# A graph-network kernel's carry pass: 86 weight columns in three groups of 32, with a fourth row tile in the fourth column group

## The chip, the cores and the metric

The kernel runs on one core of a Trainium2 chip. The metric is the device time of one execution in microseconds. The kernel before took 1119.12 us (median of 3 runs, 1116.25 to 1122.83).

## What is computed

Four graph layers run one after another on x (2708 nodes, 128 features) and a sparse-valued but densely stored matrix adj (2708 x 2708); each ends with a residual sum and a layer norm. Layer 0 is a Laplacian product with a nearest-neighbour step, layers 2 and 3 are products of adj with the features. The change lies in layer 1, an attention:

```python
XW = jnp.matmul(X, W)
s_col = jnp.matmul(XW, a[0, :f])
s_row = jnp.matmul(XW, a[0, f:])
Z1 = jax.nn.leaky_relu(s_row[:, None] + s_col[None, :], negative_slope=0.01)
den = jnp.exp(Z1)
num = jnp.matmul(A, den)
att = jnp.where(num != 0, den / jnp.where(num != 0, num, 1.0), 0.0)
H = jnp.matmul(A, jnp.matmul(att, XW))
```

Because den is the exponential of a leaky rectifier of r_i + c_j, it is the larger of two products, exp(r_i) exp(c_j) and exp(0.01 r_i) exp(0.01 c_j). Once the columns j are sorted by c_j, each row i has one place at which it changes from one form to the other. The kernel uses this to get num = A @ den without an N x N x N product.

## The kernel before

**Tiling.** The transposed adjacency is read in panels. The 2708 rows are 21 full tiles of 128 and a last one of 20 (FULL = 21, LAST = 20). The columns are six chunks (C = 6): four of 512, one of 384 and one of 276. The last six row tiles stay in SBUF (`res`, RES = 6); the first sixteen (S = 16) are streamed in groups of four by `load_panel` (L157, one DMA of 4 x 128 rows by the chunk's width) into the pool `stream`, which has three buffers with the tag strip. The 20 rows of the last tile are kept at partitions 0, 32 or 64 (`few`, L92), so that three chunks' products with them can use three different row groups of TensorE.

**The order of the work.** A scheduler orders the instructions of each engine by the dependences; the source's order is a hint, and only stretches under `manual_schedule` are kept as written. Each engine then takes its own queue in order. SyncE issues the panel loads; GpSimd issues the scatters, broadcasts and gathers.

**The third pass (L785 to L960), which the change rewrites.** The sorted columns are cut into NB = 43 blocks of 64. For a row that lies wholly on one side of a block, its contribution to that block needs only one of two weights. So lc (L786) holds for each row tile 2 x 43 = 86 weight columns, and the pass multiplies all of adj by them: `by_panels` (L171) goes over the chunks c and the row tiles i, and `product` (L180, the matmul is L186) adds lc of tile i, 128 x 86, times the panel of tile i, 128 x up to 512, into one PSUM bank for the chunk. The outputs use 86 of the 128 columns of the array. When a chunk is done, `end_carry` (L952) copies the bank to `carry`, on VectorE for even chunks and on ScalarE for odd ones (`evacuate`, L151).

**What runs beside it.** GpSimd's queue holds, in this sequence: 22 indirect scatters by_rank (L815), the load of the sorted features xws (L916), 22 scatters by_slot, the product xws * g_col (L936), the load of slots (L930), and two broadcasts of a row to all partitions by `on_all` (L806): g_row and gb. Both take the one buffer with the tag hT, so gb is written only when the last reader of g_row is done. That reader is `listed` (L938): it makes the gather's indices slot_i (L940) and 43 weight tiles lw (L947, one per block, on VectorE) from g_row. `ranked` (L928) is called after chunk 2 and `listed` after chunk 3.

**The own stage (from L989).** After a branch on a flag, for each half h of the columns and each pair of blocks q, GpSimd gathers the rows that change form within a block (L1035, indices slot_i) into a strip buffer; two rows of carry are added by SyncE (L1040); TensorE forms num from rows and lw in two groups of 64 columns (L1048); ScalarE and VectorE turn num into err (L966 to L972, the last with gb); and TensorE adds err times xws into hacc (L977). The gathers stand in GpSimd's queue behind gb, and their strip buffers are those of the panels.

Of the kernel before, what the change touches and what calls it, by code (L numbers as in the profile page):

```python
# [13 lines left out]
ALU = mybir.AluOpType  # L14
# [7 lines left out]
KC = 126  # L22
OOB = 4095
# [5 lines left out]
class Due:  # L29
# [21 lines left out]
def kernel(  # L51
# [16 lines left out]
    nc = tc.nc  # L68
    N, D = x.shape
    assert D == P  # L70
    T = (N + P - 1) // P
# [18 lines left out]
    GROUPS = 3  # L90

    def few(c):  # L92
        g = c % GROUPS * 32
        return slice(g, g + LAST)
# [37 lines left out]
    ident = const.tile([P, P], F32, tag="ident", name="ident")  # L132
# [18 lines left out]
    def evacuate(n, dst, src):  # L151
        if n % 2:
            nc.scalar.copy(dst, src)
        else:
            nc.vector.tensor_copy(dst, src)

    def load_panel(g, c, pool=stream):  # L157

        s = pool.tile([P, 4, CW], F32, tag="strip", name="part")
        nc.sync.dma_start(  # L160
            s[:, :, : cw[c]],
            adjT[g * 4 * P : (g + 1) * 4 * P, cols[c]].rearrange("(t p) k -> p t k", p=P),
        )
        return s
# [6 lines left out]
    def by_panels(weights, done, tick=None, ready=(), first=None, behind=None):  # L171

        ready = list(ready)
        accs = {}

        def product(c, i, src, w):  # L180
            lhsT = weights(i)[few(c) if i == FULL else slice(None)]
            start = c not in accs
            if start:
                accs[c] = acc_tile()
            stop = tick is None and i == (FULL if c % GROUPS == 0 else FULL - 1)
            nc.tensor.matmul(accs[c][: lhsT.shape[-1], :w], lhsT=lhsT, rhs=src, start=start, stop=stop)  # L186

        for c in range(C):
            w = cw[c]
            for i in [*(first if first and c == 0 else range(FULL)), *([FULL] if c % GROUPS == 0 else [])]:  # L190
                if i == FULL:
                    for n in range(c, c + GROUPS):
                        product(n, i, res[few(n), i - S, cols[n]], cw[n])
                    done(c, accs[c])
                    for _ in range(GROUPS if tick is not None else 0):
                        tick()
                    continue
                if i < S:
# [130 lines left out]
    with tc.tile_pool(name="knn", bufs=1) as knn:  # L329
# [96 lines left out]
        with (  # L426
# [5 lines left out]
            for c in range(C):  # L432
# [24 lines left out]
                ts = chunk_tiles[c]  # L457
# [51 lines left out]
        for n, half in enumerate((1, 0)):  # L509
# [3 lines left out]
                op0=ALU.mult, op1=ALU.mult, accum_out=wae[:, D + n : D + n + 1],  # L513
# [272 lines left out]
    lc = lc_pool.tile([P, T, NB, 2], F32, tag="lc", name="lc")  # L786

    with tc.tile_pool(name="rank", bufs=1) as rank:
        def rtile(shape, name, dt=F32):
            return rank.tile([P] + shape, dt, tag=name, name=name)  # L790
# [5 lines left out]
        def as_row(col, name):  # L796

            ps = mis_tile()
            nc.tensor.transpose(ps[:T, :P], col, ident)
            lines = rank.tile([T, P], F32, tag=name, name=name)  # L800
            nc.scalar.activation(lines, ps[:T, :P], AF.Exp, scale=0.99)
            flat = dram.tile([T, P], F32, tag=name + "_d", name=name + "_d")
            nc.gpsimd.dma_start(flat[:, :], lines)
            return flat

        def on_all(name, flat):  # L806
            row = big.tile([P, N], F32, tag="hT", name=name)
            nc.gpsimd.dma_start(row, bass.AP(tensor=flat.tensor, offset=flat.offset, ap=[[0, P], [1, N]]))
            return row
# [51 lines left out]
        with tc.manual_schedule(engines={nc.vector.engine}):  # L861
            for t0, t1 in ((0, 4), (4, half_t), (half_t, T)):
                n = t1 - t0
# [15 lines left out]
        for t0, t1 in halves:  # L879
            n = t1 - t0  # L880
# [11 lines left out]
        for t0, t1 in halves:  # L892
            rhs = in_b[:, t0:t1, :].rearrange("p t b -> p (t b)")
# [10 lines left out]
        pos = rtile([T], "pos")  # L904
# [6 lines left out]
            nc.vector.tensor_copy(val[:, :, n], v)  # L911
        nc.vector.scalar_tensor_tensor(pos, pos, float(NB), blk, op0=ALU.mult, op1=ALU.add)
        pos_u = rtile([T], "pos_u", U32)
        placed = nc.vector.tensor_copy(pos_u, pos).ins
        r_row = as_row(rr, "g_r")
        nc.gpsimd.dma_start(  # L916
            xws[:, : N // P, :], by_rank[: FULL * P, :].rearrange("(q p) d -> p q d", p=P)
# [5 lines left out]
        carry = big.tile([P, N], F32, tag="y", name="carry")  # L923
        slots = rtile([NB, 3], "slots")
        g_row = None


        def ranked():  # L928
            nonlocal g_row
            nc.gpsimd.dma_start(slots.rearrange("p b v -> p (b v)"), by_slot.rearrange("(p b) v -> p (b v)", p=P))  # L930
            with tc.issue_after(placed):
                nc.vector.tensor_copy(csort, xws[:, :, D + 1])
            nc.scalar.activation(g_col, csort, AF.Exp, scale=0.99)
            nc.scalar.activation(g_inv, csort, AF.Exp, scale=-0.99)
            g_row = on_all("g_row", as_row(csort, "g_c"))
            nc.gpsimd.tensor_mul(xws[:, :, :D], xws[:, :, :D], g_col[:, :, None].to_broadcast([P, NQ, D]))  # L936

        def listed():  # L938
            for h in range(2):
                nc.vector.tensor_scalar(  # L940
                    slot_i[h], slots[:, :, 0], 2.0, 2.0 * OOB + h, op0=ALU.mult, op1=ALU.add
                )

            nc.vector.tensor_scalar_add(slot_e, slots[:, :, 1], ident[:, KC : KC + 1])
            nc.vector.tensor_scalar_add(slot_f, slots[:, :, 2], ident[:, KC + 1 : KC + 2])
            for b in range(NB):
                nc.vector.tensor_scalar(  # L947
                    lw[:, b, : bw[b]], g_row[:, b * BJ : b * BJ + bw[b]], slot_e[:, b : b + 1], slot_f[:, b : b + 1],
                    op0=ALU.mult, op1=ALU.max,
                )  # L950

        def end_carry(c, acc):  # L952
            evacuate(c, carry[: 2 * NB, cols[c]], acc[: 2 * NB, : cw[c]])
            if c == 2:
                ranked()
            if c == 3:
                listed()

        by_panels(lambda i: lc[:, i, :, :].rearrange("p b s -> p (b s)"), end_carry)
        gb = on_all("gb", r_row)  # L960

    def mix(w, q, num, col, haccs, pool):
# [27 lines left out]
    with tc.If(over > KC) as full:  # L990

        with (
# [10 lines left out]
            for h in range(2):  # L1003
                hacc = dps.tile([P, 3 * CW], F32, tag="hacc", name="hacc")
                for q in range(NQ):
                    num = dps.tile([P, 3 * CW], F32, tag="num", name="num")
                    for i in range(T):
# [5 lines left out]
                        s = stream.tile([P, HALF], F32, tag="strip", name="part")  # L1013
                        nc.sync.dma_start(s[: pw[i]], adjT[i * P : i * P + pw[i], h * HALF : (h + 1) * HALF])
                        for c0 in range(0, HALF, CW):
# [3 lines left out]
                                start=(i == 0), stop=(i == T - 1),  # L1019
# [3 lines left out]
    with full.Else():  # L1023
        with (
# [4 lines left out]
            for h in range(2):  # L1029
                hacc = ops.tile([P, 3 * CW], F32, tag="hacc", name="hacc")  # L1030
                for q in range(NQ):
                    pair = [b for b in (2 * q, 2 * q + 1) if b < NB]
                    rows = stream.tile([P, 2, HALF], F32, tag="strip", name="rows")
# [9 lines left out]
                    for c0, w, bufs in ((0, WIDE, 2), (WIDE, NARROW, 1)):  # L1043
                        num = ops.tile([P, w], F32, tag=f"num{w}", name="num", bufs=bufs)
                        for o in range(0, w, CW):
                            e = min(w, o + CW)
                            for n, b in enumerate(pair):
                                nc.tensor.matmul(  # L1048
                                    num[n * BJ : n * BJ + bw[b], o:e], lhsT=lw[:, b, : bw[b]],
                                    rhs=rows[:, n, c0 + o : c0 + e], start=True, stop=True,  # L1050
# [9 lines left out]
    for t in range(T):  # L1060
        p = pw[t]
# [41 lines left out]
    for t in range(T):  # L1103
        p = pw[t]
# [59 lines left out]
```

## Time and profile before

| | |
|---|---|
| time, median of 3 | 1119.12 us |
| profiled span | 1119.4 us |
| mean granted TensorE clock | 0.971 |
| PE busy | 1044.2 us (93%) |
| VectorE, ScalarE, GpSimd busy | 642.7, 306.1, 299.4 us |
| first product of the third pass | 445.52 us from the start |
| last product of the third pass ends | 547.65 us |
| first gather of the own stage issued | 541.91 us |
| first hacc product of the own stage | 562.99 us |
| own stage's mT copied | 781.22 us |

A line of the profile names the source line, the engine, the operation and the tiles (out<-in), then partitions x elements and a count. PE is the matmul, PEld the loading of weights beside it, DVE is VectorE, ACT ScalarE, POOL GpSimd and SP SyncE. A float32 product is recorded as two matmul instructions and two weight loads. In a timeline the first number is the start in us from the start of the span and the second the length of the merged piece; the square bracket gives how long the engine had been idle and what ended it.

### The profile page before, as it was taken

How to read it: one execution, taken by the hardware profiler on the slowest of the kernel's cores; microseconds unless marked ns; L12 is line 12 of the kernel's file. 1: busy time of each engine (PE TensorE's matmuls, PEld its weight loads, DVE VectorE, ACT ScalarE, POOL GpSimd, SP SyncE). 2: the span in 40 equal slices, each digit the busy share in tenths (PEclk: the TensorE clock that was granted, in tenths of full speed). 3: DMA queues.
4: the chain of work that ended last, by engine and by line, in shares of the span. 5: the costliest groups of instructions: out<-in, count | busy, mean ns of one | idle time of the engine just before them, and what ended most of it. 6: DMA issues, size and time to landing. Idle time of an engine off the chain costs nothing.

```text
span 1119.4 us, 10743 instructions
## 1 busy us (share of the span) xinstructions
PE 1044.2 (93%) x3495; PEld 494.5 (44%) x3495; DVE 642.7 (57%) x1381; ACT 306.1 (27%) x569; POOL 299.4 (27%) x296
## 2 busy tenths in 40 slices
PE   0899999999999975999799999998999999999997
PEld 0346544444345654333333333333444644465445
DVE  6885549999636679403099999997311212122132
ACT  0000145555202434000165656664110100011000
POOL 4000000000477772772355655660010100000000
PEclk9999999999999995999999999998999999998999
DMA  9996320000576660797545534454475766563754
GB/s 349 354 316 222 125 101 1 1 0 1 178 274 201 184 207 13 230 304 236 164 121 148 176 96 129 164 171 142 150 236 186 227 227 219 173 227 117 263 166 129
DMA packets 110245, 193.89 MB, mean 173 GB/s; under 512 B 14156, under 2 KB 47106, under 8 KB 109926
## 3 DMA queue, kind: packets, MB, share of 16 engines
q1 hardware_dynamic: 91046, 151.12, 40.7%
q0 software_dynamic: 19136, 42.01, 12.0%
q8 instruction: 29, 0.48, 0.2%
q14 instruction: 34, 0.28, 0.1%
HBM read 217.20 MB, written 4.30 MB: 198 GB/s over the span
## 4 chain that ended last, share of the span: by engine, by line
PE 51%; issue 4%; DMA 4%; DVE 2%; POOL 1%; ACT 1%; POOLq 0%; DVEq 0%; ACTq 0%
PE acc L186 32%; PE hacc L977 8%; PE num L1048 8%; DMA rows<-in_adjT,slot_i 2%; DMA part<-in_adjT 1%; PE mis L259 1%; POOL rows L1035 1%; DVE mask L692 1%; PE mis L1110 0%; PE mis L1063 0%; DMA got<-y_rows,where 0%; ACT junk L710 0%; ACT hT L220 0%; PE mis L1076 0%; DVE mask L697 0%
## 5 line engine op out<-in xcount | busy, mean ns | idle before, releaser
L186 PE MATMUL acc<-part,y 128*128 128x512 f32 (+2 forms) x384 | 156.0, 550 | 2.1 <-DMA part<-in_adjT 1.6
L1035 POOL DMA_INDIRECT rows<-in_adjT,slot_i x86 | 120.7, 1404 | 107.9 <-PE num L1048 79.9
L1048 PE MATMUL num<-rows,lw 128*64 128x512 f32 (+2 forms) x516 | 117.0, 558 | 6.7 <-DMA rows<-carry 3.7
L977 PE MATMUL hacc<-err,xws 128*128 128x512 f32 (+3 forms) x264 | 113.6, 567 | 2.2 <-DVE err L972 1.8
L574 PE MATMUL acc<-zT,z 128*128 128x512 f32 (+4 forms) x264 | 106.9, 552 | 0.0
L602 POOL DMA_INDIRECT got<-y_rows,where x88 | 93.0, 1057 | 29.6 <-issue 11.9
L186 PEld LDWEIGHTS acc<-part,y 128*128 128x128 f32 x384 | 70.4, 191 | 64.5 <-issue 53.9
L970 DVE TENSOR_TENSOR err<-inv,num 128x1024 f32<-128x1024 f32 (+1 forms) x88 | 74.5, 856 | 27.1 <-DMA rows<-in_adjT,slot_i 21.0
L966 ACT ACTIVATE inv<-num 128x1024 f32<-128x1024 f32 (+1 forms) x88 | 64.3, 734 | 88.4 <-PE num L1048 86.6
L575 ACT COPY key<-acc 128x512 f32<-128x512 f32 (+3 forms) x132 | 70.2, 534 | 58.1 <-issue 29.8
L392 PE MATMUL acc<-part,y 128*128 128x512 f32 (+2 forms) x192 | 82.4, 582 | 2.2 <-DVE y L233 2.2
L977 PEld LDWEIGHTS hacc<-err,xws 128*128 128x128 f32 (+1 forms) x264 | 47.1, 192 | 80.4 <-issue 41.8
L186 PE MATMUL acc<-part,lc 128*86 128x512 f32 (+2 forms) x192 | 76.2, 553 | 3.3 <-DVE lc L876 2.5
L186 PE MATMUL acc<-part,xs 128*128 128x512 f32 (+2 forms) x192 | 78.6, 552 | 0.1
L972 DVE SCALAR_TENSOR_TENSOR err<-gb,g_inv,err 128x1024 f32<-128x1024 f32 (+1 forms) x88 | 77.1, 918 | 0.0
L536 POOL TENSOR_TENSOR y<-xs,d2inv 128x2176 f32<-128x2176 f32 (+1 forms) x2 | 4.6, 2322 | 264.3 <-ACT d2inv L534 264.3
L186 PE MATMUL acc<-part,mixed 128*128 128x512 f32 (+2 forms) x192 | 75.0, 545 | 0.2 <-DMA part<-in_adjT 0.2
L971 DVE SCALAR_TENSOR_TENSOR err<-err,inv 128x1024 f32<-128x1024 f32 (+1 forms) x88 | 71.8, 857 | 0.0
L574 PEld LDWEIGHTS acc<-zT,z 128*128 128x128 f32 (+1 forms) x264 | 47.0, 186 | 53.8 <-issue 48.4
L220 ACT COPY hT<-acc 128x512 f32<-128x512 f32 (+2 forms) x18 | 9.6, 534 | 220.1 <-PE acc L186 203.2
L967 ACT ACTIVATE inv<-inv 128x1024 f32<-128x1024 f32 (+1 forms) x88 | 67.3, 768 | 2.6
L576 DVE MAX8 near<-key 128x8 f32<-128x2708 f32 (+1 forms) x22 | 65.3, 2970 | 3.4 <-ACT key L575 3.4
(239 smaller groups left out, 1215.5 us busy)
## 6 DMA issues: line engine op xcount, KB each, us to landing
part<-in_adjT SPq DMA_DIRECT2D x102, 1024.0 KB
part<-in_adjT SPq DMA_DIRECT2D x24, 768.0 KB
part<-in_adjT SPq DMA_DIRECT2D x24, 552.0 KB
res<-in_adjT SPq DMA_DIRECT2D x4, 1280.0 KB
got<-y_rows,where POOLq DMA_INDIRECT x88, 3.9
rows<-in_adjT,slot_i POOLq DMA_INDIRECT x86, 5.8
rows<-carry SPq DMA_DIRECT2D x86, 10.6 KB
xws<-by_rank POOLq DMA_DIRECT2D x1, 1365.0 KB, 10.1
```

Source lines behind the costliest of these rows:

```text
L186: nc.tensor.matmul(accs[c][: lhsT.shape[-1], :w], lhsT=lhsT, rhs=src, start=start, stop=stop)
L392: nc.tensor.matmul(accs[c][:, : cw[c]], lhsT=y[:, i, :], rhs=src[:, : cw[c]], start=first, stop=last)
L574: nc.tensor.matmul(pks[c][:p, : cw[c]], lhsT=z2[:, :p], rhs=zT[:, cs], start=False, stop=True)
L575: nc.scalar.copy(key[:p, cs], pks[c][:p, : cw[c]])
L602: nc.gpsimd.indirect_dma_start(out=got[:p, :], out_offset=None, in_=y2_rows[:, :], in_offset=bass.IndirectOffsetOnAxis(ap=where[:p, t, k : ...
L967: nc.scalar.activation(inv[:p], inv[:p], AF.Exp, scale=-1.0)
L970: nc.vector.tensor_mul(err[:p], inv[:p], num[:p, :w])
L971: nc.vector.scalar_tensor_tensor(err[:p], err[:p], 2.0, inv[:p], op0=ALU.subtract, op1=ALU.mult)
L972: nc.vector.scalar_tensor_tensor(err[:p], gb[:p, col : col + w], g_inv[:p, q : q + 1], err[:p], op0=ALU.max, op1=ALU.mult)
L977: nc.tensor.matmul(haccs[:, o:e], lhsT=xws[:p, q, :D], rhs=err[:p, o:e], start=(q == 0), stop=(q == NQ - 1))
L1035: nc.gpsimd.indirect_dma_start(out=rows[:KC, n, :], out_offset=None, in_=adj_half[:, :], in_offset=bass.IndirectOffsetOnAxis(ap=slot_i[h][ ...
L1048: nc.tensor.matmul(num[n * BJ : n * BJ + bw[b], o:e], lhsT=lw[:, b, : bw[b]], rhs=rows[:, n, c0 + o : c0 + e], start=True, stop=True,)
```

## The change

The 86 weight columns are cut into three groups, 32, 32 and 22 wide, each of which goes to its own column group of the array: output partitions 0 to 31, 32 to 63 and 64 to 85. The fourth column group, partitions 96 to 127, is then free, and takes a fourth row tile: while row tiles 1, 2 and 3 of a panel are each multiplied in three groups, one third of the fourth tile goes through the fourth group each time. So four row tiles are meant to take the time of three products. Since the three thirds of the fourth tile all come out at partitions 96 to 127, they need three PSUM banks: the chunk's own and two more, taken from the pool mis.

At the end of a chunk the bank is copied to carry on ScalarE, and VectorE adds the three parts from partitions 96 up. `listed` moves from chunk 3 to chunk 4 and makes only the first 10 of the 43 lw tiles; the other 33 come after the adds of the last chunk. `issue_after` keeps csort, slot_i and lw behind the adds on VectorE.

```diff
-        def listed():
-            for h in range(2):
...
-            for b in range(NB):
+        def listed(added):
+            with tc.issue_after(added):
+                for h in range(2):
...
+            weigh_own(range(NB // 4))
+
+        def weigh_own(blocks):
+            for b in blocks:
                 nc.vector.tensor_scalar(
                     lw[:, b, : bw[b]], g_row[:, b * BJ : b * BJ + bw[b]], slot_e[:, b : b + 1], slot_f[:, b : b + 1],
                     op0=ALU.mult, op1=ALU.max,
                 )
 
-        def end_carry(c, acc):
-            evacuate(c, carry[: 2 * NB, cols[c]], acc[: 2 * NB, : cw[c]])
+        lcs = lc.rearrange("p t b s -> p t (b s)")
+        Q = 32
+        quads = [slice(o, min(o + Q, 2 * NB)) for o in range(0, 2 * NB, Q)]
+        assert len(quads) == 3
+        left = [slice(3 * Q, 3 * Q + q.stop - q.start) for q in quads]
+        banks, begun = {}, set()
+
+        def part_sum(c, i, src, bank, rows, k):
+
+            if (c, bank) not in banks:
+                banks[c, bank] = mis_tile() if bank else acc_tile()
+            nc.tensor.matmul(
+                banks[c, bank][rows, : cw[c]], lhsT=lcs[:, i, quads[k]], rhs=src,
+                start=(c, bank, rows.start) not in begun, stop=False, skip_group_check=True,
+            )
+            begun.add((c, bank, rows.start))
+
+        for c in range(C):
+            for g in range(T // 4 + 1):
+                ts = range(4 * g, min(4 * g + 4, FULL))
+                part = load_panel(g, c) if g < S // 4 else None
+                srcs = [
+                    part[:, i % 4, : cw[c]] if part is not None else res[:, i - S, cols[c]] for i in ts
+                ]
+                for n, i in enumerate(ts[:3]):
+                    for k in range(3):
+                        part_sum(c, i, srcs[n], 0, quads[k], k)
+                    if len(ts) == 4:
+                        part_sum(c, ts[3], srcs[3], n, left[n], n)
+            if c % GROUPS == 0:
+                for n in range(c, c + GROUPS):
...
+            nc.scalar.copy(carry[: 2 * NB, cols[c]], banks[c, 0][: 2 * NB, : cw[c]])
+            for bank, (q, r) in enumerate(zip(quads, left)):
+                added = nc.vector.tensor_add(carry[q, cols[c]], banks[c, bank][r, : cw[c]], carry[q, cols[c]])
             if c == 2:
-                ranked()
-            if c == 3:
-                listed()
-
-        by_panels(lambda i: lc[:, i, :, :].rearrange("p b s -> p (b s)"), end_carry)
+                ranked(added.ins)
+            if c == 4:
+                listed(added.ins)
+            if c == C - 1:
+                with tc.issue_after(added.ins):
+                    weigh_own(range(NB // 4, NB))
         gb = on_all("gb", r_row)
```

More of the change, by code (lines that the diff above doesn't have):

```diff
@@ L913 @@
         pos_u = rtile([T], "pos_u", U32)
-        placed = nc.vector.tensor_copy(pos_u, pos).ins
+        nc.vector.tensor_copy(pos_u, pos)
         r_row = as_row(rr, "g_r")
@@ L925, with ranked @@
         g_row = None
-        def ranked():
+        def ranked(added):
             nonlocal g_row
             nc.gpsimd.dma_start(slots.rearrange("p b v -> p (b v)"), by_slot.rearrange("(p b) v -> p (b v)", p=P))
-            with tc.issue_after(placed):
+            with tc.issue_after(added):
                 nc.vector.tensor_copy(csort, xws[:, :, D + 1])
@@ L936, in ranked @@
             nc.gpsimd.tensor_mul(xws[:, :, :D], xws[:, :, :D], g_col[:, :, None].to_broadcast([P, NQ, D]))
-        def listed():
-            for h in range(2):
[L940 to L945, printed above, removed]
-            for b in range(NB):
+        def listed(added):
+            with tc.issue_after(added):
+                for h in range(2):
+                    nc.vector.tensor_scalar(
+                        slot_i[h], slots[:, :, 0], 2.0, 2.0 * OOB + h, op0=ALU.mult, op1=ALU.add
+                    )
+                nc.vector.tensor_scalar_add(slot_e, slots[:, :, 1], ident[:, KC : KC + 1])
+                nc.vector.tensor_scalar_add(slot_f, slots[:, :, 2], ident[:, KC + 1 : KC + 2])
+            weigh_own(range(NB // 4))
+        def weigh_own(blocks):
+            for b in blocks:
                 nc.vector.tensor_scalar(
@@ new lines @@
+        banks, begun = {}, set()
[5 more added lines that the diff above has]
+                start=(c, bank, rows.start) not in begun, stop=False, skip_group_check=True,
+            )
+            begun.add((c, bank, rows.start))
[13 more added lines that the diff above has]
+                for n in range(c, c + GROUPS):
+                    if n != c:
+                        banks[n, 0] = acc_tile()
+                    nc.tensor.matmul(
+                        banks[n, 0][: 2 * NB, : cw[n]], lhsT=lcs[few(n), FULL, :], rhs=res[few(n), FULL - S, cols[n]],
+                        start=n != c, stop=False, skip_group_check=True,
+                    )
+                    begun.update((n, 0, q.start) for q in quads)
+            nc.scalar.copy(carry[: 2 * NB, cols[c]], banks[c, 0][: 2 * NB, : cw[c]])
+            for bank, (q, r) in enumerate(zip(quads, left)):
+                added = nc.vector.tensor_add(carry[q, cols[c]], banks[c, bank][r, : cw[c]], carry[q, cols[c]])
+            if c == 2:
+                ranked(added.ins)
[4 more added lines that the diff above has]
+                    weigh_own(range(NB // 4, NB))
```

## The prediction

> **What bounds the kernel now.** The page first: PE is busy 93% of the span and the chain that ended last gives PE 51%, so what counts in a stage is whether TensorE works back to back there. Then its list of costly groups, for the group the change rewrites:
>
> ```profile
> L186 PE MATMUL acc<-part,lc 128*86 128x512 f32 (+2 forms) x192 | 76.2, 553 | 3.3 <-DVE lc L876 2.5
> ```
>
> That is the third pass, panel tiles only (the resident tiles are another group). Each product is two instructions. The timeline gives its pace, the windows what TensorE and the DMA engines do meanwhile (columns: stretch, length, busy us of PE, PEld, DVE, ACT, POOL, granted clock, DMA share, GB/s):
>
> ```profile
> 503.93 13.90 PE L186 MATMUL acc<-part,lc 128*86 128x512 f32 x32
> ```
>
> ```profile
> 452.00:468.00 16.00, 16.00 (x44) 5.58 (x43) 9.46 (x29) 1.68 (x5) 12.56 (x12) 1.00 0.91 292
> 468.00:486.00 18.00, 18.00 (x43) 6.53 (x42) 0.82 (x2) 0.33 (x2) 12.38 (x13) 1.00 0.84 278
> 486.00:504.00 18.00, 18.00 (x44) 6.49 (x43) 0.00 (x0) 0.58 (x1) 13.81 (x15) 1.00 0.90 284
> 504.00:523.00 19.00, 19.00 (x49) 6.54 (x47) 4.20 (x19) 0.27 (x1) 6.32 (x4) 1.00 0.78 261
> 548.00:563.00 15.00, 9.46 (x31) 3.04 (x31) 4.60 (x6) 6.91 (x10) 5.24 (x6) 0.89 0.37 107
> ```
>
> TensorE never rests from 452 to 537, but DMA is at 78 to 91% behind it: there is little more speed in this pass before the panels are late. After the pass (its last matmul ends at 547.65) PE does 9.5 us of work in 15 us. So next I read who starts the own stage, in the queue of GpSimd and in the chain:
>
> ```profile
> 513.12 0.55 POOL L808 DMA_DIRECT2D g_row<-g_c_d  x1 [3.34 <-DMA g_c_d<-g_c]
> 529.95 0.54 POOL L808 DMA_DIRECT2D gb<-g_r_d  x1 [16.28 <-DVE lw L947]
> 541.91 1.11 POOL L1035 DMA_INDIRECT rows<-in_adjT,slot_i  x1 [11.42 <-DMA part<-in_adjT]
> ```
>
> ```profile
> 538.73 3.01 DMA part<-in_adjT
> ...
> 541.91 0.38 POOL rows L1035
> ...
> 546.09 11.52 DMA rows<-in_adjT,slot_i
> ```
>
> The first gather waits for the last panel (landed 541.74), and the gathers, not the matmuls of the pass, lead to the first hacc product at 562.99 (timeline of PE), 21.1 us after the gather was issued. One line of the queue matters most: gb stands ahead of the gathers and waits 16.28 us for lw, because gb takes the buffer (tag hT) of g_row, which lw reads. Today lw is over in time:
>
> ```profile
> 520.00 9.65 DVE L947 TENSOR_SCALAR lw<-g_row,slot_e,slot_f 128x64 f32<-128x64 f32 x43 [6.13 <-DMA g_row<-g_c_d]
> ```
>
> **What the Trainium skill says.** "TensorEngine Tiling (Array Packing)", Tiling Modes: four tiles of 128 rows by 32 columns run independently, and a change of mode drains the array. The trace has two and three tiles at once: of the 20-row products of three column chunks, the first passes all start at 466.67 and the second at 467.17; 64-column pairs of num start two by two at 604.47 and 604.90.
>
> ```profile
> 466.67 0.67 PE L186 MATMUL acc<-res,lc 20*86 20x512 f32 x3
> ```
>
> ```profile
> 604.90 0.60 PE L1048 MATMUL num<-rows,lw 128*64 128x512 f32 x2
> ```
>
> "TensorE: Matmul & The Clock Gate", Part 3, measured 3.07x for four row tiles and 2.38x for three column tiles, each as one lone pack; no run here has four at once. "DMA: Bandwidth & Descriptors", Anatomy of one DMA, prices a GpSimd DMA at 2.0 us plus bytes over 436 GB/s: 5.2 us for the 1.39 MB of gb. Here g_row took 6.9 us beside panels (513.12 to 520.00).
>
> **The change part by part.** (1) *Products.* A pass is 13.90 / 32 = 0.43 us, a product 0.86 us for 512 columns, and by columns 0.64 for 384 and 0.46 for 276. One row tile over all six chunks: 4 x 0.86 + 0.64 + 0.46 = 4.54 us. 21 full tiles are 95 us today. In groups of four, 5 x 3 + 1 = 16 sets are 73 us if four tiles run as fast as one: 22.7 us less. The bounds of a set are 1 product (the pairs above) and 4 / 3.07 = 1.30 (lone pack, an estimate from that page). I take 1, since at 2 and 3 tiles no pass is longer than 0.50.
>
> (2) *What the pass gives back.* In the built order of the changed kernel, the fourth tile's parts of banks 1 and 2 come late in chunk 0 (they want mis buffers that the place and totals products hold): seven of them then queue on the fourth column group. My count for chunk 0: two sets to 449.0 as two products now (the granted clock is 0.60 from 440 to 452), 0.9 for totals and place, 5 sets, 0.7 for the second totals and place and a transpose (454.9), 7 sets bound by the fourth group, 7 more, and two separate times 1.05 for the 20-row products, which now stand in two places: 469.0, where the chunk ends at 467.70 today. Then 13.7 for chunk 1 and for chunk 2; 16.6 for chunk 3 (again a late set, a transpose, two places for the 20 rows), 10.3 and 7.4: the last product ends at 530.7, 17 us earlier than 547.65.
>
> (3) *Panels.* Strip 0 is freed by its last part, now near 457.5 (today the next panel is issued at 451.67). DMA busy time from 452 to 541.7, share times length, is about 75.6 us, of which gb is some 4, and gb now comes later: 71 us of work from 457.5 reach 528.5 without a gap, and 3.2 us of product remain then. That gives 531.7 at 100%, so I set the end of the pass at T3 = 533.
>
> (4) *Evacuation.* One ACT copy (0.38 for 276 columns today) and three DVE adds in place of one copy: by the ge rows (TENSOR_TENSOR, 294 elements, 0.46) about 0.43 each, 1.3 in all. For chunks 0 to 4 they lie under the next chunk's products; DVE is idle there (0.00 of 18 us). For the last they are on the path: T3 + 1.75.
>
> (5) *lw.* Ten blocks after chunk 4, the other 33 after the adds of chunk 5. At 9.65 / 43 = 0.224 they take 7.4 us: lw ends at T3 + 9.2. Queued behind: gb on GpSimd (0.3 to notice, as 529.65 to 529.95), and behind gb the branch and the gathers, whose first goes at about T3 + 10.3 instead of 541.91. Its data share GpSimd's queue with gb, whose 1.39 MB needs 3.6 us from T3 + 10: some 2 us more than the 1.2 us it takes today. First hacc at T3 + 10.3 + 2 + 21 = T3 + 33.3.
>
> (6) slots is asked for ahead of the xws product and waits for the last scatter (median 5.0 us to landing): g_row comes some 4 us later than 520, near 524. Free, since chunk 4 ends about then.
>
> Sum: 533 + 33.3 = 566.3 against 562.99, +3.3 us; from there the two kernels are alike. 1119.12 + 3.3 = **1122.5**. The break-even is T3 = 529.7: the pass must end 18 us earlier only to pay for the 16 us by which gb and the gathers move behind it and the 2 us of gb's data.
>
> **The rivals.** *Faster:* late parts do not queue, the 20 rows overlap, panels keep up. Then chunk 0 ends at 449.9 + 14 x 0.857 + 0.7 + 2.1 = 464.7, chunk 3 takes 15.2, T3 = 525.0 and hacc starts at 558.3; and if the gathers' data pass beside gb's, 556.3: 6.7 us less, 1112.5. For it: all groups started together above, and 3 us of DMA gaps can close. Against: DMA at 0.91. *Starved:* four panels and the scatters do not come at 100% of DMA; at 93% the 71 us are 76, T3 near 538, +8.5: 1128. For it: 0.84 to 0.91 is reached only with three strips waiting. *Packing costs what a lone pack does:* 0.30 x 72.6 = 22 us more, partly over the starved time, T3 near 552, +22: 1141. For it: eight weight loads a set where there are two; against: the 20-row products load six in 0.24 us.
>
> **How the numbers follow.** Forecast 0.45, faster 0.20, starved 0.20, packing 0.15. Range 1112 to 1134: it leaves out the last and a tail below. Within 0.5% is 1113.5 to 1124.7: that is the forecast's case with a little of its neighbours, 0.45; faster 0.20, slower 0.35.
>
> **What would show it.** Groups of 12 products of 32 columns in 2.6 us for 512 columns show step 1 right; more than 3.0 is the packing rival. The end of the pass read from PE, and waits for part in it, show 2 and 3. In GpSimd's queue gb must wait for lw until about 9 us after the last product, and the first gather follow it at once: if it goes before the pass ends, step 5 is wrong and the kernel some 15 us faster. PE should be idle for about 17 us between the pass and num.

## The result and the profile after

| | before | after |
|---|---|---|
| time, median (runs) | 1119.24 us (4) | 1130.99 us (4) |
| profiled span | 1119.4 us | 1127.8 us |
| copy of the last chunk starts | 547.68 us | 544.31 us |
| first gather issued | 541.91 us | 555.93 us |
| first hacc product | 562.99 us | 574.89 us |
| own stage's mT copied | 781.22 us | 789.71 us |

The ratio is 1.0104, 95% interval 1.0066 to 1.0142: the change makes the kernel 1% slower. In the profiled runs the pass ends 3.4 us earlier and the first hacc comes 11.9 us later; by the copy of mT 3.4 of these are made up, and 8.5 remain. The medians lie 11.75 us apart, the two profiled runs only 8.4: the one before took 1121.1 us, 1.8 above its median, the one after 1129.5, 1.5 below.

The group that the change rewrites (its panel tiles, chunk's own bank, then the banks of the fourth tile's parts; the columns are as in the line of before):

```profile
L969 PE MATMUL acc<-part,lc 128*32 128x512 f32 (+5 forms) x480 | 64.8, 568 | 10.3 <-DMA part<-in_adjT 7.8 <-DVE lc L876 2.5
L969 PE MATMUL mis<-part,lc 128*32 128x512 f32 (+5 forms) x96 | 41.5, 558 | 0.0
```

The wait for panels is 7.8 us now. Before it was 0.8, all of it in the last chunk:

```profile
L186 PE MATMUL acc<-part,lc 128*86 128x276 f32 x32 | 7.8, 399 | 0.8 <-DMA part<-in_adjT 0.8
```

(The two busy times overlap: two products in different column groups run at once.) A panel of four full row tiles in the timeline of TensorE, with no wait in it:

```profile
470.35 1.48 PE L969 MATMUL acc<-part,lc 128*32 128x512 f32 x11
471.25 0.59 PE L969 MATMUL mis<-part,lc 128*32 128x512 f32 x1
471.66 0.60 PE L969 MATMUL acc<-part,lc 128*32 128x512 f32 x3
471.68 0.59 PE L969 MATMUL mis<-part,lc 128*32 128x512 f32 x1
...
472.94 1.46 PE L969 MATMUL acc<-part,lc 128*32 128x512 f32 x11
```

The next panel starts 2.59 us after this one (470.35 to 472.94), where four products took some 3.5 (eight passes of 0.43). From 471.25 on a set of three of the chunk's bank and one of mis starts every 0.43 us: the packing works as meant. Next the windows of the pass from chunk 2 to chunk 5 (stretch, length, busy us of PE, PEld, DVE, ACT, POOL, granted clock, DMA share, GB/s):

```profile
484.80:502.45 17.65, 14.62 (x131) 3.91 (x134) 2.08 (x3) 0.58 (x2) 13.31 (x14) 1.00 1.03 331
502.45:521.00 18.55, 18.55 (x135) 4.85 (x133) 2.26 (x4) 1.19 (x5) 9.73 (x8) 1.00 0.68 227
521.00:535.56 14.56, 12.37 (x133) 4.47 (x133) 2.08 (x3) 0.58 (x1) 0.00 (x0) 0.88 0.75 252
535.56:544.31 8.75, 7.57 (x124) 3.77 (x116) 4.63 (x17) 0.47 (x1) 0.00 (x0) 1.00 0.28 84
```

Read the DMA share beside the busy time of PE. In chunk 2 the DMA engines are full and TensorE waits 3.0 us. In chunk 3 TensorE is busy throughout and DMA falls to 0.68, since all three strips hold panels that are not used up: SyncE's four loads in this chunk wait 15.8 us in total for the fourth tile's products, the last readers of a strip (total, times, longest):

```profile
SPq L160 <- PE mis L969: 15.8, 4, 8.4
```

In chunk 4 TensorE waits again, and its clock is 0.88. What the DMA could have carried in chunk 3 was not carried ahead. Over the whole pass, from the first load after strip 0 is free to the end of TensorE's last wait for a panel:

```profile
457.60:540.80 83.20, 75.37 (x665) 21.98 (x656) 17.78 (x42) 3.40 (x8) 41.03 (x39) 0.98 0.82 273
```

The last wait for a panel ends at 540.80, where the last panel before had landed at 541.74. So TensorE's faster products brought the panels hardly any sooner.

In GpSimd's queue, the lines that answer to those of before:

```profile
517.95 0.56 POOL L808 DMA_DIRECT2D g_row<-g_c_d  x1 [2.71 <-DMA g_c_d<-g_c]
553.88 0.55 POOL L808 DMA_DIRECT2D gb<-g_r_d  x1 [35.38 <-DVE lw L951]
555.93 1.10 POOL L1081 DMA_INDIRECT rows<-in_adjT,slot_i  x1 [1.49 <-issue]
```

and what gb waits for, on VectorE:

```profile
545.20 0.93 DVE L998 TENSOR_TENSOR carry<-mis,carry 32x276 f32<-32x276 f32 x2
546.17 7.42 DVE L951 TENSOR_SCALAR lw<-g_row,slot_e,slot_f 128x64 f32<-128x64 f32 x33
```

gb's idle time before it has grown from 16.28 to 35.38 us, and the first gather is issued 11.6 us after the last chunk's copy began, where it went 5.8 us ahead of it before. TensorE then stands still until the rows are there:

```profile
562.18 1.94 PE L1094 MATMUL num<-rows,lw 128*64 128x512 f32 x2 [17.93 <-DMA rows<-in_adjT,slot_i]
```

### The profile page after: what moved, and what is told of

Read it like the earlier page. It is cut to its first block, busy times and chain, and to the rows that moved or that the text cites. A ratio compares the mean times of both kernels' runs of the same rounds, so it can differ in the third digit from the quotient of the medians.

```text
span 1127.8 us, 11773 instructions
## 1 busy us (share of the span) xinstructions
PE 1028.4 (91%) x3999; PEld 478.4 (42%) x3999; DVE 651.8 (58%) x1396; ACT 307.8 (27%) x572; POOL 299.5 (27%) x296
## 3 DMA queue, kind: packets, MB, share of 16 engines
q0 software_dynamic: 19136, 42.01, 11.9%
## 4 chain that ended last, share of the span: by engine, by line
PE 42%; issue 7%; DMA 3%; POOL 1%; DVE 1%; ACT 1%; POOLq 0%; DVEq 0%
PE acc L186 24%; PE hacc L1023 8%; PE num L1094 8%; DMA rows<-in_adjT,slot_i 2%; PE mis L259 1%; DMA part<-in_adjT 1%; POOL rows L1081 1%; PE mis L1156 0%; PE mis L1109 0%; ACT hT L220 0%; PE mis L1122 0%; PE mis L1152 0%; DVE err L1017 0%; ACT mT L1099 0%; DVE err L1018 0%
## 5 line engine op out<-in xcount | busy, mean ns | idle before, releaser
L186 PE MATMUL acc<-part,y 128*128 128x512 f32 (+2 forms) x384 | 154.5, 546 | 2.2 <-DMA part<-in_adjT 1.6
L392 PE MATMUL acc<-part,y 128*128 128x512 f32 (+2 forms) x192 | 79.5, 566 | 3.2 <-DVE y L233 2.2
L969 PE MATMUL acc<-part,lc 128*32 128x512 f32 (+5 forms) x480 | 64.8, 568 | 10.3 <-DMA part<-in_adjT 7.8
L1094 PEld LDWEIGHTS num<-rows,lw 128*64 128x64 f32 (+1 forms) x516 | 36.6, 137 | 82.4 <-issue 62.9
```

What stands on the lines that cost most here:

```text
L392: nc.tensor.matmul(accs[c][:, : cw[c]], lhsT=y[:, i, :], rhs=src[:, : cw[c]], start=first, stop=last)
L1094: nc.tensor.matmul(num[n * BJ : n * BJ + bw[b], o:e], lhsT=lw[:, b, : bw[b]], rhs=rows[:, n, c0 + o : c0 + e], start=True, stop=True,)
```

## The experiments

Two figures are read from each profiled run: where the last chunk's copy to carry begins (T), and what follows it to the end of the span. They separate the pass from the tail: 571.7 us follow T before, 583.5 after. The theory was: a faster pass that is starved of panels, and a tail that is 12 us longer by the queue lw, gb, gathers. The first three sets of runs were on three other chips, on which the kernel before itself takes 1154 to 1164 us (in the profiled runs there the third pass starts 34 to 42 us later than on the first chip). So their ratios are against their own runs of the kernel before, and their stretches are compared with one another. No trace of the kernel before is kept from these chips.

**The late lw alone, on the products of before.** As in the change, `listed` follows chunk 4; its copy and the last chunk's are on VectorE, so that lw can stand behind them.

```diff
-            for b in range(NB):
+            weigh_own(range(NB // 4))          # after chunk 4
+        # after the last chunk's copy:
+        weigh_own(range(NB // 4, NB))
```

> The kernel before, products untouched, with only the change's handling of lw: slot_i and 10 lw tiles after chunk 4's copy, 33 after the last chunk's copy (that copy and chunk 4's on VectorE). Queue theory: last copy near 548.3, lw until 555.8, gb at 556.1, first gather near 558 instead of 541.9: +16, time 1135. Rival (the products' end sets the start, and it is the same here): 1119 to 1120.

Measured: 1174.0 us, ratio 1.0155 (1.0095 to 1.0216), some 19.5 us over the 1154.5 of before. T is 586.4, and 581.0 us follow it. The queue of GpSimd, run with the late lw alone:

```profile
594.48 0.54 POOL L808 DMA_DIRECT2D gb<-g_r_d  x1 [41.37 <-DVE lw L950]
596.53 1.11 POOL L1045 DMA_INDIRECT rows<-in_adjT,slot_i  x1 [1.51 <-issue]
```

The same wait on lw stands here with the old products, and 9.3 us more follow T than before on the first chip: most of the tail's 11.8 us belongs to lw's place, not to the packing. The time was to grow by 16 us. Where the rest of the 19.5 lies, the traces don't show; the profiled run, the fastest of the four, is 14.6 over.

**lw all after chunk 4; gb in another buffer; half the panels.** Three edits of the changed kernel:

```diff
-            weigh_own(range(NB // 4))
+            weigh_own(range(NB))              # the call after the last chunk goes
```

```diff
-        gb = on_all("gb", r_row)              # tag hT, shared with g_row
+        gb = wide.tile([P, N], F32, tag="wide", name="gb")
+        nc.gpsimd.dma_start(gb, ...)
-    mT = wide.tile([P, N], F32, tag="wide", name="mT")
+    mT = big.tile([P, N], F32, tag="hT", name="mT")
```

```diff
-                part = load_panel(g, c) if g < S // 4 else None
+                if g % 2 == 0 ...: part = load_panel(g, c)   # panels 0 and 2 only, each used twice
```

> The changed kernel with all 43 lw tiles made after chunk 4's adds, ahead of the last chunk's adds. Queue theory (the own stage starts when the last lw lets gb go, and the gathers stand behind gb): lw ends near 548 instead of 553.6, gb goes near 548.4 and the first gather near 550.4 instead of 555.9; time 1131.0 - 5.5 = 1125.5. Rival, the end of the pass (last product, evacuation, TensorE's clock after its rest) sets the start: the last adds come some 4 us later than now, so 1131 to 1135.

> The changed kernel with gb in the buffer of xwe (tag wide) and mT in the buffer of g_row (tag hT): gb no longer waits for lw, and goes ahead of the by_slot scatters. Queue theory: the first gather follows the last panel, which lands at 541 now and some 2 to 4 us later with gb's 1.39 MB among the panels; first gather 543 to 545, first hacc product near 565 instead of 574.9; time near 1121. Rival (end of the pass sets the start): no gain, 1131 to 1134.

> The changed kernel loading only panels 0 and 2 of each chunk in the third pass and using each of them twice: the same products on half the panel bytes (the panels 1 and 3 are left out, so carry holds other sums). Theory that late panels cost the pass 13 us: waits for part vanish, TensorE stays at full clock, the last product ends at 531 to 533 instead of 544.3, the first gather goes near 543, time near 1119.5. Rival, that the column groups themselves (late parts, four groups at once, weight loads) fill the pass: last product near 544, time near 1131.

Measured: 1188.8 us, ratio 1.0265 (1.0191 to 1.0340); 1193.5, 1.0332 (1.0264 to 1.0399); 1185.9, 1.0239 (1.0175 to 1.0302). Without a run of the changed kernel beside them these could not be placed, so the last two were run again with it, and with a kernel that broadcasts g_row twice:

```diff
             g_row = on_all("g_row", c_row)
+            nc.gpsimd.dma_start(g_row, ...)   # the same 1.39 MB again
```

> The changed kernel as it is, run beside the next three as their control, because the first call had none and landed on a chip where the kernel before alone takes 1154 us. Every theory: about 1.0% above the kernel before where the chip runs as in the first measurement (ratio 1.004 to 1.016); if instead the chip is the slow one of the first call, about the 1.025 to 1.035 that its three variants of the changed kernel showed there, which would mean that those edits gained nothing.

> The changed kernel with gb in a buffer of its own, so that its broadcast needn't wait for the late lw and nothing stands ahead of the gathers on GpSimd. Queue theory: gathers start when the strip buffers come free, right after the last product (T3), not 9.6 us after it; the end moves 8 to 10 us earlier than the changed kernel's, to a ratio of about 1.00 against the kernel before. Rival (the own stage is bound by its gathers' bandwidth, or gb's broadcast takes the panels' bandwidth instead): T3 itself moves 3 to 6 us later because the broadcast now runs beside the panels, and no more than 4 us is gained.

> The changed kernel with only panels 0 and 2 of every chunk loaded, each used for two groups of row tiles (so the third product is of other data). Panels theory (waits for panels, and the half clock that follows a wait, are what separates T3 = 544 from the 531 to 533 of my count): T3 falls to 529 to 534 on a chip like that of the first measurement, and the end comes 10 to 14 us earlier than the changed kernel's (ratio about 1.00). Rival (the PE is itself slower than my count: late parts, more and narrower instructions): T3 stays within 3 us of 544 and the ratio near 1.01.

> The changed kernel with g_row's broadcast (1.39 MB) issued a second time right behind the first, into the same buffer. Collision theory (the broadcast takes the DMA engines from the panels of chunk 4): the wait for the panel in chunk 4 grows by 3 to 5 us, and T3 and the end come 3 to 6 us later than the changed kernel's. Rival (panels have slack there and the pass is set by the PE): the wait grows by less than 1 us and the end stays within 2 us.

| kernel | time, us | ratio (95%) | chunk 1's copy to T, us | T to end, us |
|---|---|---|---|---|
| changed | 1192.8 | 1.0292 (1.0238 to 1.0346) | 52.4 | 583.3 |
| gb in another buffer | 1191.3 | 1.0248 (1.0202 to 1.0294) | 56.0 | 571.7 |
| half the panels | 1184.5 | 1.0187 (1.0132 to 1.0243) | 48.1 | 586.2 |
| g_row twice | 1202.4 | 1.0360 (1.0317 to 1.0403) | 60.3 | 583.2 |
| lw all after chunk 4 (on the chip of the first set) | 1188.8 | 1.0265 (1.0191 to 1.0340) | 52.8 | 575.9 |

In the four runs beside one another the third pass starts at 479.7, 485.1, 487.9 and 487.3 us, though what is edited comes after that. So the stretches say more than the times.

*The tail.* With gb in another buffer 571.7 us follow T, as before the change on the first chip, against 583.3 in the changed kernel beside it; with lw out of the way 575.9. The match is in part luck: ScalarE's last copy starts 2.1 us after the last product here (616.6 to 618.7), elsewhere at once, so from the last product on it is 573.8. Of the 11.8 us, then, 9.5 to 11.6 are lw's and gb's. But the time did not fall by that, a miss: T came 13.5 us later than in the changed kernel beside it. Of these, 5.3 are there when the pass starts, 4.6 more come by the end of chunk 1 (562.7 against 552.7), and 3.2 in chunk 5 (11.9 us against 8.7), of which the late copy has 2.1. In GpSimd's queue gb is issued early, and stands ahead of the scatters of by_slot, waiting for its data (run with gb in another buffer):

```profile
523.87 0.58 POOL L1007 DMA_DIRECT2D gb<-g_r_d  x1 [10.29 <-DMA g_r_d<-g_r]
```

The last scatter is issued at 551.6 instead of 537.4. A wait was taken from one place in the queue and put in another; that it is what makes chunks 0 and 1 longer is likely but not shown.

*The panels.* With half of them the stretch from chunk 1's copy to T is 48.1 us on both chips; it is 52.4 in the changed kernel beside it and 59.5 after the change on the first chip. The time fell by 8.3 us, less than the 10 to 14 expected, and in the profiled run, the slowest of its four, T hardly moved (604.8 against 605.2): the pass had started 8.2 us later. The windows of chunks 2 to 5, half the panels:

```profile
556.66:570.39 13.73, 13.73 (x129) 5.12 (x124) 2.08 (x3) 0.58 (x1) 0.00 (x0) 1.00 0.47 152
570.39:586.88 16.49, 16.04 (x134) 4.48 (x131) 2.26 (x4) 1.19 (x4) 6.00 (x3) 1.00 0.34 104
586.88:597.36 10.48, 10.48 (x134) 4.16 (x137) 2.08 (x3) 0.59 (x2) 0.00 (x0) 1.00 0.50 168
597.36:604.79 7.43, 7.37 (x124) 3.92 (x116) 4.61 (x17) 0.47 (x1) 0.00 (x0) 1.00 0.05 11
```

TensorE alone needs 13.7, 10.5 and 7.4 us for chunks 2, 4 and 5: against 17.65, 14.56 and 8.75 after the change on the first chip, 9.3 us are panels. TensorE's idle time in these three windows, 6.4 us, is the part that needs no comparison across chips. In the changed kernel beside the half one the three take 13.9, 11.3 and 8.7, so only 2.2 us are panels there. Its chunks 0 and 1 take 73.0 us, and that panels had time to come ahead in them is my reading. Chunk 3 is another matter: 18.55 us with TensorE busy all the time, on both chips. There the scheduler left four parts of the fourth tile to run alone (first chip)

```profile
511.13 1.88 PE L969 MATMUL mis<-part,lc 128*32 128x512 f32 x4
```

and the 20-row products in two places, which it did not do with half the panels (16.49 us).

*The broadcast.* A second g_row costs 9.7 us of time, more than the 3 to 6 expected; 7.1 us of that stand in chunk 4 (18.35 us against 11.26 in the changed kernel beside it), while 3.9 us of T's delay are there by chunk 1's copy. TensorE's wait for the panel in that chunk, changed kernel of the first profile and then g_row twice:

```profile
529.09 1.75 PE L969 MATMUL acc<-part,lc 128*32 128x384 f32 x11 [2.19 <-DMA part<-in_adjT]
```

```profile
601.29 2.13 PE L971 MATMUL acc<-part,lc 128*32 128x384 f32 x11 [5.62 <-DMA part<-in_adjT]
```

It grew from 0.58 in the changed kernel beside it to 5.62. And a wait costs more than itself. The passes that follow the 2.19 us in the first profile:

```profile
530.02 0.85 PE L969 MATMUL mis<-part,lc 128*32 128x384 f32 x1
...
533.41 0.49 PE L969 MATMUL mis<-res,lc 128*32 128x384 f32 x1
```

0.85 against 0.49 us for the same operation: the granted clock fell to 0.56 (529.09 to 532.54), and the panel took 3.45 us, where the ones before it took 1.94.

**What made these chips cost the change 33 us, not 12.** In the changed kernel there chunks 0 and 1 took from 479.7 to 552.7 us, with the old products (late lw alone) from 484.5 to 525.3: 73.0 against 40.8. TensorE's waits in the changed kernel (total, times, longest) are one for a panel, which SyncE asked for only at 506.5, and several without a releaser ("issue"):

```profile
PE acc L969 <- DMA part<-in_adjT: 8.8, 1, 8.8
PE mis L969 <- issue: 7.8, 4, 5.3
```

The longest, 5.3 us, ends at 495.67. It may be a wait for a bank of mis: ScalarE's late copy of totals, which frees one, ended at 495.61, and with gb in another buffer the profile puts the wait at this place, 7.9 us, down to that copy. The waits from 528 to 541, with a DMA share of 0.03 or less up to 540, have no such reason in sight. Two explanations were tested: three times as many products (12 for a panel instead of 4) outrun the supply of instructions, or packing is slow in itself. So: chunks 0 and 1 in whole products of 86 columns, only 2 to 5 packed; the same with each whole product cut in three pieces of columns (as many products as the packed ones, no packing); and the first with a mended tail.

```diff
+                if c < 2:
+                    for n, i in enumerate(ts):
+                        nc.tensor.matmul(banks[c, 0][: 2 * NB, : cw[c]], lhsT=lcs[:, i, :], rhs=srcs[n], ...)
+                    continue
```

```diff
+                        for o in range(0, cw[c], 176):    # three pieces
+                            nc.tensor.matmul(banks[c, 0][: 2 * NB, o:e], lhsT=lcs[:, i, :], rhs=srcs[n][:, o:e], ...)
```

```diff
-            g_row = on_all("g_row", as_row(csort, "g_c"))
+            g_row = on_all("g_row", as_row(csort, "g_c", nc.scalar), nc.scalar)   # ScalarE's queue
-            if c == 4: listed(added.ins)       # and 33 lw after the last chunk
+            if c == 3: listed(added.ins)       # all 43 lw here; gb in its own buffer
```

> The changed kernel, but chunks 0 and 1 use the 86 columns in one product as the kernel before did, and only chunks 2 to 5 are packed: 80 fewer products on TensorE, all in the stretch in which GpSimd still scatters. Theory of the instruction supply (where the chip feeds its engines slowly, 12 short products per panel instead of 4 long ones starve TensorE while the scatters run): on such a chip chunk 1 ends at about 525 us as with the products of the kernel before, instead of 549 to 563, the last product comes 48 to 53 us after it, and the run lands at 1158 to 1166, ratio 1.00 to 1.007. On a chip like that of the first measurement the two chunks are bound by panels anyhow and nothing changes by more than 3 us (ratio about 1.008). Rival (the packing is slow in itself, also in chunks 2 to 5, or the stall only moves on to chunk 2): ratio stays at 1.02 to 1.03 on the slow chip.

> The run above with each product of chunks 0 and 1 cut into three pieces of up to 176 of its 512 columns: no packing there, weights of all 86 columns, but exactly as many products as in the changed kernel (three for each row tile). Supply theory: chunk 1 ends at 545 us or later on a chip that feeds slowly, as with the packed products, and the run is 20 us or more above the run above. Rival (it is packing, not the number of instructions): at most some 6 us above the run above, for weight loads that a shorter product no longer hides (each product some 0.13 to 0.2 us a load, two loads).

> The first of these runs with the tail mended too: g_c and g_row go out by ScalarE's queue (not behind GpSimd's scatter and slots), all lw are made after chunk 3, and gb has its own buffer and is fetched after chunk 4. Queue and collision theory: the gathers start before the last product as in the kernel before, so the stretch from the last product to the end falls from 583.4 to about 571.5 us; g_row lands in the stretch of chunk 3 in which the panel buffers are full, so chunk 4 loses 2 to 4 us; the run is 13 to 16 us faster than the first of these runs, and 0.5 to 1.2% faster than the kernel before. Rival (what is gained at the tail goes into collisions of gb with the panels of chunk 5, or of g_row with those of chunk 3): less than 8 us under the first of these runs.

| kernel | time, us | ratio (95%) | chunk 1's copy | chunk 2's copy | T | T to end |
|---|---|---|---|---|---|---|
| first chunks whole | 1183.1 | 1.0185 (1.0103 to 1.0267) | 528.8 | 556.0 | 594.9 | 582.5 |
| first chunks cut | 1198.6 | 1.0287 (1.0202 to 1.0372) | 558.2 | 572.2 | 611.1 | 585.4 |
| whole and tail | 1183.6 | 1.0183 (1.0103 to 1.0263) | 523.0 | 557.6 | 606.0 | 568.7 |

TensorE's waits from 484 to 560, first chunks cut, and then first chunks whole (total, times, longest):

```profile
PE acc L988 <- issue: 20.5, 23, 1.7
```

```profile
PE acc L969 <- issue: 3.4, 5, 1.1
```

Cutting brings the stall back with no packing at all (chunk 1's copy at 558.2 against 528.8), far beyond the 6 us that uncovered weight loads were to cost: on this chip the number of products is enough to bring it on. (The waits named "issue" are less than the stall: in the changed kernel, pieces of two and three short passes are recorded as 1.9 and 2.0 us long between them.) My forecast for the whole ones, 1158 to 1166, was a miss: the stall moved on, as the rival said. Chunk 2, now the first packed one, took 27.2 us instead of some 14. In the changed kernel, the whole and the cut one the stall ends about when GpSimd's scatters end (the last issued at 537.4, 546.5 and 540.6). The whole run with the mended tail gained 13.8 us after T (568.7 against 582.5) and lost 11 before it, 2.4 of them by the same late last copy: TensorE's waits for panels were 11.8 us instead of 1.8, and chunks 2 and 3 took 34.6 and 24.1 us instead of 27.2 and 18.6.

**The last run.** No packed product beside the scatters, gb fetched late by another queue:

```diff
-                if c < 2:
+                if c < 3:
...
+            if c == 4:
+                gb = wide.tile(...); nc.scalar.dma_start(gb, ...)   # after chunk 4's copy
```

> The changed kernel with chunks 0 to 2 in products of all 86 columns and only 3 to 5 packed, so that no packed product runs while GpSimd still scatters; gb has its own buffer and goes out by ScalarE's queue after chunk 4's copy. Theory that short products starve only while the scatters last: on a chip that feeds slowly chunk 2 ends near 545 us, no wait without a releaser stands in chunks 3 to 5, they take 38 to 40 us as they did there before (18.5, 11.4 and 8.8), the last product ends at 583 to 585, and with 571.7 us after it the run lands at 1153 to 1158, ratio 0.992 to 1.00. On a chip like that of the first measurement: chunk 2 ends at 502 to 503, the last product at 541 to 544, the end at 1113 to 1117, ratio 0.994 to 0.998. Rival (the first hundred or so short products starve wherever they stand): chunk 3 takes 27 us or more instead of 18.5, and the run lies 8 us or more above the kernel before.

This chip is like that of the first measurement (before: 1119.5). Measured: 1121.0 us, ratio 1.0017 (1.0001 to 1.0033): most of the change's 1% is back, and nothing is won on the kernel before. After T 570.2 us follow, as wanted. The windows of chunks 2 (whole) to 5:

```profile
487.74:505.77 18.03, 18.03 (x46) 6.31 (x48) 0.00 (x0) 0.58 (x1) 13.52 (x14) 1.00 0.92 299
505.77:522.03 16.26, 16.26 (x137) 4.34 (x140) 0.77 (x2) 0.60 (x4) 6.62 (x4) 1.00 0.74 236
522.03:534.17 12.14, 10.68 (x133) 4.04 (x134) 2.08 (x3) 0.58 (x2) 0.00 (x0) 1.00 0.88 278
534.17:549.39 15.22, 9.23 (x124) 4.25 (x116) 4.62 (x17) 0.47 (x2) 5.89 (x6) 0.78 0.66 207
```

Chunks 3 and 4 take 28.4 us, 4.7 less than in the changed kernel. Chunk 5 takes 15.2 instead of 8.8, and the timeline of TensorE says why:

```profile
544.21 1.59 PE L969 MATMUL acc<-part,lc 128*32 128x276 f32 x11 [5.92 <-DMA part<-in_adjT]
```

gb (asked for at 534.5) and four gathers (from 537.5) are issued before that panel arrives, and share the DMA engines with it. That takes T to 549.4, past the 541 to 544 that I expected; 3 of these us were lost by the end of chunk 2 (505.8 instead of 502 to 503). No wait without a releaser stands in its chunks 3 to 5; since the changed kernel shows none on the first chip either, that does not decide whether the scatters are what starves short products elsewhere.

## Why the prediction came out as it did

The forecast of 1122.5 us was 8.5 too low: no measurable change was its likeliest case, and the kernel is 1% slower. The 1131.0 lie in the range, nearer to the starved rival's 1128. The mechanism was right, and one step was far off in size; that the sum came no further out is partly luck. In the profiled runs the forecast's +3.3 us became 8.5 by an end of the pass 11.3 too late, a stretch to hacc 2.7 shorter than forecast, and 3.4 made up after it.

- **Products (step 1): right.** A set takes one product time: a panel in 2.59 us against 2.6 forecast. The rival that priced a set at 1.30 is out.
- **What the pass gives back (step 2): right but for one term.** 13.7, 10.3 and 7.4 us for chunks 2, 4 and 5 stand in the run with half the panels, on another chip, as 13.73, 10.48 and 7.43. Chunk 3 was put at 16.6 and takes 18.55 with no wait: its lone fourth parts and the second place of the 20-row products were priced 2 us too low. Chunks 0 and 1 together are 2.1 late, of which 1.45 are waits for panels.
- **Panels (step 3): the step that failed.** T3 was put at 533 and is 544.3. The term is the 71 us of DMA work that were to run "without a gap". The work was sized about right: 0.82 of the 83.2 us from 457.60 to 540.80 are some 68 us. The gaps, some 15 us, were priced at next to nothing: 1.3 us between the 531.7 "at 100%" and 533. They come because with all three strips full the loads stop, as in chunk 3 (share 0.68); and what wasn't loaded then can't be made up when the strips are empty, as in chunk 2, where TensorE waits at a share of 1.03. Of the 13.6 us between the count of 530.7 and 544.3, chunk 2 has 3.9, chunk 4 has 4.3 and chunk 5 has 1.35, and with the 1.45 of chunks 0 and 1 panels have some 11; chunk 3's lone parts have 1.95. The starved rival, T3 at 538, had the right cause and still too small a size.
- **g_row later (step 6): the 4 us were near** (517.95 against 513.12 for the issue, 4.8), "free" was wrong. It moved towards the panels of chunk 4, and the second broadcast shows that they pay for one that falls on them; what the first costs by itself was not measured.
- **Evacuation and lw (steps 4 and 5): right in mechanism, near in size.** The adds end 1.8 us after T (1.75 forecast), lw 9.3 (9.2), the first gather goes at 11.6 (10.3), hacc follows at 30.6 (33.3). The 2 us for gb's data beside the gathers don't show: from the first gather to hacc it is 19.0 us, where it was 21.1 before and 23 were forecast. Taken alone, with the old products, the late lw costs 9.3 us after T; with gb's wait undone the stretch after T goes back to 571.7 (573.8 from the last product).
- **"From there the two kernels are alike": nearly.** 11.9 us at the first hacc are 8.5 at mT. Of these 3.4, 1.9 are made up by the first copy of mT (673.40 and 683.40 us) and 1.5 after it. There TensorE's products are the same and its busy time is 1.5 us less, at a mean clock of 1.00 instead of 0.98, which owes nothing to the change as far as the traces show.

The break-even reads: the pass had to end 18 us earlier to pay for the tail. Measured by what follows T, the tail costs 11.8. The pass ended 3.4 us earlier: of the 17 us in my count, 13.6 went to panels that came late and to the parts that run alone.

## What to carry to other kernels

A faster engine draws on the buffers behind it: count its supply chunk by chunk against the buffers it has, since a mean DMA share over a stage hides that full buffers stop the loads and empty ones stop the engine. When a late producer writes or reads a shared buffer, follow the queue of whoever waits for that buffer: here a load that nobody needed yet held up the gathers behind it, worth more than the pass gained. Moving such a load elsewhere is no sure gain. Three of these runs moved it: in the first two the pass ended about as much later as the tail got shorter, and in the last, where gb and the gathers share the DMA engines with the last panel, a wait of 5.9 us for that panel took back about half.

## What was not expected of the hardware

- Four column groups in a steady stream run as fast as one: 12 products in 2.59 us, 3 product times. "TensorE: Matmul & The Clock Gate", Part 3, of the Trainium skill has 3.07x measured for a pack of four row tiles and 2.38x for one of three column tiles; this stream shows no such loss.
- What many short products cost differs between chips. The changed kernel lies 1.0% above the kernel before on the first chip and 2.9% on another. In its first two chunks there, part of TensorE's waits have no releaser, and three pieces for one product were enough to bring such waits on: 20.5 us in 23 waits. That slow supply of instructions is the cause is inferred from this. ScalarE was late there too (its copy of totals starts some 6 us after the product that it reads), and a late panel, perhaps also a late bank, are part of the packed kernel's stall. That the scatters take part was not shown, and a kernel without them was not tried. Each chip was used for one set of runs, so whether the difference is the chip's own is open.
